# Turning normed tokens and key features through a DRAM scratch and VectorE's 32x32 blocks, in a window-attention plus linear-attention plus recurrence kernel

## The chip, the core and the metric

The kernel runs on one core of one Trainium2 chip, in float32 throughout. A core has TensorE (PE, matrix products; its weight loads are listed apart as PEld), VectorE (DVE), ScalarE (ACT), GpSimd (POOL) and SyncE (SP, which here only issues DMA transfers). The metric is the device time of one execution in microseconds (us), taken as the median of several runs.

## What is computed

The input is `x` with shape (16, 56, 56, 128): 16 images of 56x56 = 3136 tokens with 128 channels. Cut to what matters:

```python
# layer 0: shifted 7x7 window attention, 4 heads of 32, on a group-normed image
x = x + window_attention(group_norm(x)) @ w_out + b_out
# layer 1, on tokens t of shape (16, 3136, 128)
n = layer_norm(t)                      # over the 128 channels
q, k, v = split(n @ W.T + b)           # 128 channels each
q, k = elu(q) + 1, elu(k) + 1          # the "features"
num = q_t . cumsum_t(k_t v_t^T);  den = q_t . cumsum_t(k_t)
t = t + num / (den + 1e-6)             # causal linear attention
m = layer_norm(t) @ Wf.T               # second norm
m = batch_norm(m) * gamma + beta       # over all 16*3136 tokens
y_t = sigmoid(m_t + V y_{t-1})         # recurrence over the tokens of an image
out = t + y
```

Both layer norms give normed tokens with tokens on the partitions. The products that follow need them with channels on the partitions, so each normed group has to be turned. The causal attention also needs the key features both ways: channels on partitions for the products with the queries, tokens on partitions for the running state `sum k v^T`.

## The kernel before

Images are worked one after the other, with overlap. An image is cut into 8 rows of windows (`window_row`) and 7 token groups (`token_group`): six full groups of 512 tokens (four chunks of 128) and a small one of 64. For a token group the work is:

- `project` (L1132, PE) and `plus_attention` (L1141, DVE) finish layer 0 in the token buffer `xt_buf`.
- `layer_scale` with key `a` makes the normed tokens: `stats` (L1031, DVE), `join` (L1038 to L1045, POOL), `scale` (L1051, POOL) into `xn`, then `turn`: four 128x128 PE transposes into a PSUM bank (by the helper at L620). `x_out` (L1160, ACT) copies the bank to `xnT`.
- `feature(1)` and `feature(0)` make key and query features `f1`, `f0`: product (L1173, PE), relu and exp (L1183, L1192, ACT), `larger` (L1196, DVE). `values` (L1221, PE) and `v_out` (L1230, DVE) make `v_buf`.
- `turn_k` (L1244, PE, four transposes) and `k_out` (L1248, ACT) give `k`, the key features with tokens on partitions. `products` (L1259, PE) multiplies keys with queries: `f1` is the operand that is loaded as weights.
- `attend` (L1288, L1291, PE) and `gather` (L1299, PE) use and extend the running state, which `copy_state` (L1311, ACT) takes out of PSUM after each chunk; `update` (L1368, DVE) adds the result to `xt_buf`, and `store` (L1092, SP) writes it to DRAM.
- `layer_scale` with key `f` does the second norm in the same way; `xf_out` (L1384, ACT) copies to `xfT`, `whole` (L1388, PE) multiplies, `xs_out` (L1405, ACT) lays the result into `staged`, and `store_inputs` (L1426, SP) writes one image of it to DRAM.

For images 1 to 15 the group norm's channels-first image is not made by PE: `load_turned` (L322, SP) loads the image into one of two buffers `spare` so that VectorE can turn it in 32x32 blocks (L654, seven instructions per image). After all images a second stage runs the recurrence over stored inputs (L1657 to L1722).

The order of the first stage is written by a planner. Each step has an engine, a cost and a delay in us (literals in the code), the steps it follows, and buffers that it takes and drops. `Plan.emit` runs a list schedule forwards and backwards up to 200 times with its own costs, keeps the shortest plan and emits all steps by planned start. On the chip each engine then works through its fixed order and waits where an input or a buffer is not ready; SP's transfers are in such a fixed order too. The steps compete for a few buffers: three PSUM banks (`b`), two pairs of banks (`a`), two `xn`, one each of `xnT`, `xfT`, `f0`, `f1`.

Of the kernel before, what the change touches and what calls it, by code (L numbers as in the profile page):

```python
# [11 lines left out]
ALU = mybir.AluOpType  # L12
# [14 lines left out]

TOL2 = 2.0 ** -38


# [24 lines left out]
class Plan:  # L55
# [97 lines left out]
    def forwards(self, rank):  # L153


        left = {tag: [(k, None) for k in range(n)] for tag, n in self.bufs.items()}
        users, where, behind = {}, {}, {}
        for s in self.steps:
            for d in s.drops:
                users.setdefault(d, []).append(s)  # L160
        count = {d: len(u) for d, u in users.items()}

        def begin(s):
            takes = [d for d in s.takes if d not in where]
            if not all(left[d.tag] for d in takes):
                return False
            for d in takes:
                where[d], before = left[d.tag].pop(0)
                if before is not None:
                    behind.setdefault(s.n, []).extend(users[before])  # L170
            return True

        def done(s):
            for d in s.drops:
                count[d] -= 1
                if not count[d]:
                    left[d.tag].append((where[d], d))

        start, end = self.run(
            [s.missing for s in self.steps],  # L180
            [s.then for s in self.steps],
            rank,
            [0.0] * len(self.steps),
            begin,
            done,
        )
        if any(t is None for t in start):
            return None
        return start, end, where, behind
# [16 lines left out]
    def emit(self):  # L206
        best = now = self.forwards([s.rank for s in self.steps])
        assert best is not None
        for i in range(self.PASSES):
            back = self.backwards(*now[:2], now[3], self.AHEAD[i % len(self.AHEAD)])  # L210
            now = self.forwards([-t for t in back])
            if now is None:
                break
            if now[1] < best[1]:
                best = now
        start, self.span, where, _ = best
        for d, place in where.items():
            d.place = place

        for s in sorted(self.steps, key=lambda s: start[s.n]):  # L220
            s.emit()
# [3 lines left out]
def tile_conv_attn_hybrid(  # L225
# [52 lines left out]
    x3_d = dram.tile([B * T, C], F32, name="x3_d")  # L278
    xs_d = dram.tile([NJ, P, B - 1, KB, NCH], F32, name="xs_d")


# [133 lines left out]
    with ExitStack() as s1:  # L415
# [14 lines left out]
        def own(buf, *shape):  # L430
# [4 lines left out]
            return owned[key]  # L435

        NQ2 = 64 + WT
        psum = bass.MemoryType.PSUM
# [45 lines left out]
        for xt in xt_bufs:  # L484
# [6 lines left out]
                **{f"xt{i}": 1 for i in range(3 * NG)},  # L491
                "spare": 2,
                "oT": 1,
# [55 lines left out]
        def load(b, rank, paced):  # L549
# [17 lines left out]
            for g in range(NG):  # L567
# [12 lines left out]
                def emit(g=g):  # L580
# [4 lines left out]
                        "SP",  # L585
                        2.0 if g < NG - 1 else 0.7,
                        rank + g,
                        emit,
                        after,
                        takes=[bufs[g]],  # L590
                        lag=6.0,
                    )
# [6 lines left out]
        def load_turned(b, rank):  # L599

            buf = Buf("spare")
            parts = []
            for q in range(4):
                parts.append(
                    plan.step(
                        "SP",
                        5.0,
                        rank + q,
                        lambda q=q: load_blocks(b, spare[buf.place], q),
                        [issued, *parts[-1:]],  # L610
                        takes=[buf],
                        lag=12.0,
                    )
                )
            return buf, parts
# [22 lines left out]
        def turned(b, t, loaded, xw_buf, rank):  # L638
# [10 lines left out]
            for j in range(NG if b else 0):  # L649
                rk = rank + SLOT * 6.0 * j / NG  # L650

                def turn_rows(j=j):
                    n = R * W
                    nc.vector.transpose(  # L654
                        image_rows(xw_buf)[:, R * j : R * (j + 1), 0:W],
                        flat(spare[xp.place])[:, n * j : n * (j + 1)],
                    )
# [358 lines left out]
        last_pd = [[], []]  # L1016
        chain = {"state": None, "kept": None, "buf": None, "project": None, "turn": None}

        def layer_scale(t, g, d, key, rank, after, drops=()):

# [3 lines left out]

            end = key == "f" and t["b"] == B - 1 and g >= NG - 2

            def stats():
# [20 lines left out]

            def scale():
                d["xn"] = own(xn, P, G, C)[:, :nk]  # L1050
                (nc.vector if end else nc.gpsimd).tensor_tensor(  # L1051
                    d["xn"][:np],
                    xg,
                    d["rs"].unsqueeze(2).to_broadcast([np, nk, C]),
                    ALU.mult,
                )

            def turn():
# [5 lines left out]

            xn, bt = Buf("xn"), Buf("b")
            s = plan.step("DVE", part(g, (0.78, 0.87), (0.20, 0.28)), rank, stats, after)
# [9 lines left out]
                drops=drops,  # L1076
            )
            s = plan.step(
                "PE",
# [6 lines left out]
            )  # L1086
            return s, bt, sc

        def store(b, g, t, done, xt_buf, rank):

            def emit():
# [6 lines left out]
                    "SP",  # L1098
                    part(g, 2.0, 0.7),
                    rank,  # L1100
                    emit,
                    [done],
                    drops=[xt_buf],
                    lag=5.5,
                )
            )

        def token_group(b, g, i, t, turned_x, rows_done, oT_buf, xt_buf, rank):
# [46 lines left out]
            s = st("DVE", part(g, (0.61, 0.69), (0.20, 0.28)), rank, plus_attention, [s0, s1], drops=[bo])  # L1155
            s, bt, scaled = layer_scale(t, g, d, "a", rank, [s])

            def x_out():
                d["xnT"] = own(xnT, P, GT)
                nc.scalar.copy(d["xnT"][:, :nt], d["pt"])  # L1160

            xnT = Buf("xnT")
            xo = st("ACT", part(g, (0.47, 0.58), (0.11, 0.22)), rank, x_out, [s], takes=[xnT], drops=[bt])

            def feature(j):
# [3 lines left out]
                def proj():  # L1171
# [3 lines left out]
                        awc_sb[:, j * P : (j + 1) * P],  # L1175
                        d["xnT"][:, :nt],
                        start=True,
# [16 lines left out]
                def larger():  # L1194
                    d[key] = own(f, P, GT)
                    nc.vector.scalar_tensor_tensor(  # L1196
                        d[key][:, :nt],
                        d[f"p{j}"],
                        bqk_one[:, j : j + 1],
                        d[f"r{j}"],  # L1200
                        ALU.add,
                        ALU.max,
                    )
# [13 lines left out]
            def values():  # L1217
                pv = bank(bv, P, nk, C)
                d["pv"] = pv[:np]
                for cc in range(nk):  # L1220
                    nc.tensor.matmul(  # L1221
                        pv[:, cc, :],
                        chunk(d["xnT"], cc),
                        awc_sb[:, 2 * P : 3 * P],
# [21 lines left out]
            def k_out():  # L1246
                d["k"] = own(k, P, G, C)
                nc.scalar.copy(d["k"], d["pk"])  # L1248

            bk, k, bA, A = Buf("b"), Buf("k"), Buf("b"), Buf("A")  # L1250
            if g < NG - 1:
                s = st("PE", (0.44, 0.61), rank, turn_k, [fk], takes=[bk], drops=[bfk])
# [3 lines left out]
            def products():  # L1256
                d["pA"] = bank(bA, P, nk, np)
                for cc in range(nk):
                    nc.tensor.matmul(  # L1259
                        d["pA"][:, cc, :],  # L1260
                        chunk(d["f1"], cc),
                        chunk(d["f0"], cc)[:, :np],
# [116 lines left out]
            store(b, g, t, up, xt_buf, rank)  # L1379
            s, bt, scaled = layer_scale(t, g, df, "f", rank, [up], [xt_buf])  # L1380

            def xf_out():
                d["xfT"] = own(xfT, P, GT)[:, :nt]
                nc.scalar.copy(d["xfT"], df["pt"])  # L1384

            def whole():
                d["pw"] = bank(bw, P, nt)
                nc.tensor.matmul(d["pw"], fwTc_sb, d["xfT"], start=True, stop=True)  # L1388

# [18 lines left out]

            last = b == B - 1 and g == NG - 1
            bw, xfT = Buf("b"), Buf("xnT" if last else "xfT")  # L1410
            s = st("ACT", part(g, (0.47, 0.58), (0.11, 0.22)), rank, xf_out, [s], takes=[xfT], drops=[bt])
            s = st("PE", part(g, (0.86, 1.02), (0.17, 0.33)), rank, whole, [s], takes=[bw], drops=[xfT])
# [11 lines left out]
        def store_inputs(b, t, done, rank):  # L1424
            def emit():
# [5 lines left out]
            return plan.step(  # L1431
                "SP", 5.8, rank, emit, done, drops=[t["xs_buf"]], lag=10.0
            )
# [75 lines left out]
        def fetch(kind, m, first, last, after, tag=None):  # L1509
            def emit():  # L1510
                if tag is not None and tag[:2] == "xt":
                    ahead[kind][m] = xt_bufs[int(tag[2:])]
                elif tag is not None:
                    ahead[kind][m] = {
                        "spare": spare,
                        "xw": xw_bufs,
# [6 lines left out]
            elif tag[:2] == "xt":  # L1523
                takes = [Buf(f"xt{NG * int(tag[2:]) + g}") for g in range(NG)]
            else:
                takes = [Buf(tag)]
# [5 lines left out]
        def xs_until(b):  # L1532
# [4 lines left out]
            (M2, f"xt{(B - 2) % 3}"),  # L1537
            (0, "spare"),
            (1, "spare"),
        )  # L1540
# [333 lines left out]
```

## Time and profile before

| what | us |
|---|---|
| median of 3 runs | 1758.76 (1757.2 to 1760.62) |
| the profiled execution | 1757.42 |
| its span, first to last instruction | 1755.6 |
| first stage (0 to 1592): PE, PEld busy | 1572.39, 1302.99 |
| first stage: DVE, ACT, POOL busy | 1207.82, 1125.62, 1148.60 |
| recurrence (1592 to 1755.6): DMA share | 0.95 |

The granted TensorE clock is 0.996 of full speed. A row of instruction groups in the profile reads: line, engine, operation, output and inputs by name, shapes and count, then total busy us and mean ns of one, then the engine's idle time just before and who ended it. A duration is from start to end of one instruction; instructions of an engine overlap in part, so the distance between two starts can be well below the duration. "DMA share" is the mean busy share of the 16 DMA engines.

### The profile page before, as it was taken

Reading aid. Unit: us, or ns where it says so; the run is one execution under the profiler, and the core shown is the slowest. Engines: PE = TensorE matmul, PEld = TensorE weight load, DVE = VectorE, ACT = ScalarE, POOL = GpSimd, SP = SyncE. Lnnn points to the kernel's source line nnn. Section 1 sums busy time; section 2 is a strip of 40 time slices with the busy share of each in tenths; the row PEclk is TensorE's granted clock in tenths of the full one; section 3 lists DMA queues with packets and bytes.
Section 4 is the critical chain, followed back from the end, with each engine's and each line's share of the span. In section 5 each row is a group of like instructions: output and inputs, shape, how many; then the busy total and the mean of one; then the engine's idle time right before and its main releaser. Section 6 shows DMA issues by size and latency. Waiting matters only on the chain.

```text
span 1755.6 us, 63643 instructions
## 1 busy us (share of the span) xinstructions
PE 1719.7 (98%) x26539; PEld 1419.7 (81%) x26539; DVE 1350.2 (77%) x3174; ACT 1230.0 (70%) x3026; POOL 1152.7 (66%) x2042
## 2 busy tenths in 40 slices
PE   7999999999999999999999999999999999999997
PEld 6888888888878888888888888888888888786875
DVE  5888687686868687776878687777868677767997
ACT  5676676777767677767677677767677676766764
POOL 6887777767768687767777687768767676662000
PEclk9999999999999999999999999999999999999998
DMA  8244323132323223131323223231211020357999
GB/s 176 52 94 97 65 71 74 40 88 56 89 56 77 68 69 71 47 92 45 91 54 76 63 67 72 64 83 38 70 37 59 20 89 26 119 172 295 400 419 367
DMA packets 340391, 180.38 MB, mean 103 GB/s; under 512 B 194560, under 2 KB 323840, under 8 KB 338304
## 3 DMA queue, kind: packets, MB, share of 16 engines
q1 hardware_dynamic: 338512, 175.46, 33.9%
q8 instruction: 210, 3.44, 0.8%
q10 hardware_dynamic: 1584, 0.79, 0.1%
q14 instruction: 85, 0.70, 0.1%
HBM read 100.76 MB, written 75.46 MB: 100 GB/s over the span
## 4 chain that ended last, share of the span: by engine, by line
PE 89%; DVE 5%; DMA 3%; issue 2%; POOL 1%; ACT 1%; SPq 0%; DVEq 0%; POOLq 0%; ACTq 0%
PE bank L835 10%; PE bank L1173 10%; PE bank L856 7%; PE pair L880 6%; PE pair L935 5%; PE bank L620 5%; PE pair L954 5%; PE state_bank L1299 5%; PE bank L1259 5%; PE bank L1132 5%; PE pair L1288 5%; PE bank L1221 5%; PE pair L1291 5%; PE bank L1388 5%; PE bank L1244 2%; PE z_buf L1669 2%
## 5 line engine op out<-in xcount | busy, mean ns | idle before, releaser
L925 POOL TENSOR_TENSOR p_buf<-p_buf,rc 128x784 f32<-128x784 f32 x128 | 194.7, 1522 | 101.4 <-DVE rc L922 52.5
L906 POOL TENSOR_TENSOR s<-s,mx 128x784 f32<-128x784 f32 x128 | 192.5, 1504 | 60.8 <-DVE mx L903 56.4
L1173 PE MATMUL bank<-xnT,awc_sb 128*128 128x512 f32 (+1 forms) x448 | 210.1, 550 | 1.2 <-issue 1.2
L1183 ACT ACTIVATE r<-bank,bqk_neg 128x512 f32<-128x512 f32 (+1 forms) x224 | 142.6, 637 | 96.7 <-PE bank L1173 81.1
L1196 DVE SCALAR_TENSOR_TENSOR f<-bank,bqk_one,r 128x512 f32<-128x512 f32 (+1 forms) x224 | 150.2, 671 | 73.6 <-ACT r L1192 39.1
L1288 PEld LDWEIGHTS pair<-state,f 128*128 128x128 f32 x768 | 124.7, 191 | 45.1 <-issue 27.0
L920 DVE TENSOR_REDUCE sm<-p_buf 128x16 f32<-128x784 f32 x128 | 122.6, 958 | 45.3 <-ACT p_buf L916 44.8
L1291 PE MATMUL pair<-v_buf,A 128*128 128x129 f32 x800 | 155.3, 275 | 2.0 <-issue 1.8
L1299 PE MATMUL state_bank<-v_buf,k 128*128 128x129 f32 x768 | 153.8, 282 | 0.7 <-ACT k L1248 0.5
L891 DVE TENSOR_TENSOR s<-pair,wmask_sb 128x784 f32<-128x784 f32 x128 | 123.1, 962 | 40.5 <-PE pair L880 32.8
L1299 PEld LDWEIGHTS state_bank<-v_buf,k 128*128 128x128 f32 x768 | 122.4, 191 | 36.4 <-issue 21.6
L1288 PE MATMUL pair<-state,f 128*128 128x129 f32 x768 | 151.7, 279 | 0.0
L1311 ACT COPY state<-state_bank 128x129 f32<-128x129 f32 x384 | 105.9, 276 | 62.3 <-PE state_bank L1299 55.0
L945 ACT COPY pT<-pair 128x904 f32<-128x904 f32 x128 | 118.2, 923 | 28.7 <-PE pair L935 25.7
L1672 ACT ACTIVATE y_a<-z_buf,bsh 128x256 f32<-128x256 f32 (+1 forms) x218 | 103.3, 474 | 45.9 <-PE z_buf L1669 41.9
L1121 POOL TENSOR_TENSOR xt_buf<-xt_buf,bout_sb 128x512 f32<-128x512 f32 (+1 forms) x112 | 129.7, 1161 | 5.7 <-DMA xt_buf<-in_x_dram 5.7
L1192 ACT ACTIVATE r<-r 128x512 f32<-128x512 f32 (+1 forms) x224 | 131.0, 585 | 2.2
L1669 PE MATMUL z_buf<-y_a,fvT_sb 128*128 128x256 f32 (+1 forms) x432 | 129.7, 385 | 0.5 <-ACT y_a L1672 0.4
L880 PEld LDWEIGHTS pair<-kT,q_buf 32*49 32x49 f32 x8192 | 105.5, 120 | 27.5 <-issue 15.3
L620 PE MATMUL bank<-ident,xn 128*128 128x128 f32 x800 | 124.9, 274 | 2.1 <-issue 1.0
L1291 PEld LDWEIGHTS pair<-v_buf,A 128*128 128x128 f32 x800 | 121.5, 192 | 3.3 <-issue 2.4
L880 PE MATMUL pair<-kT,q_buf 32*49 32x49 f32 x8192 | 121.8, 206 | 2.3 <-issue 2.3
(159 smaller groups left out, 4773.0 us busy)
## 6 DMA issues: line engine op xcount, KB each, us to landing
x_d<-xt_buf SPq DMA_DIRECT2D x96, 256.0 KB, 2.3
xt_buf<-in_x_dram SPq DMA_DIRECT2D x93, 256.0 KB, 2.8
spare<-in_x_dram SPq DMA_DIRECT2D x60, 392.0 KB, 4.6
xs_d<-staged SPq DMA_DIRECT2D x15, 1568.0 KB, 6.5
out_dram<-xw_buf SPq DMA_DIRECT2D x6, 1792.0 KB, 19.2
x_ring<-x_d SPq DMA_DIRECT2D x5, 1792.0 KB, 16.9
xw_buf<-x_d SPq DMA_DIRECT2D x4, 1792.0 KB, 14.8
out_dram<-x_ring SPq DMA_DIRECT2D x4, 1792.0 KB, 17.0
```

The costliest lines, as they stand in the source:

```text
L620: nc.tensor.transpose(pt[:, CK * cc : CK * (cc + 1)], xg[:, cc, :], ident)
L835: nc.tensor.matmul(d[key], wqkv_sb[:, j * P : (j + 1) * P], xk, start=True, stop=True)
L880: nc.tensor.matmul(sc[64 * hh : 64 * hh + WT, hp, w * WT : (w + 1) * WT], qT[r : r + HD, w * WT : (w + 1) * WT], d["kT"][r : r + HD, w * W ...
L906: nc.gpsimd.tensor_tensor(d["sf"], d["sf"], d["mx"].unsqueeze(2).to_broadcast([P, nb, WT]), ALU.subtract,)
L925: nc.gpsimd.tensor_tensor(prf, prf, d["rc"].unsqueeze(2).to_broadcast([P, nb, WT]), ALU.mult)
L1173: nc.tensor.matmul(d[f"p{j}"], awc_sb[:, j * P : (j + 1) * P], d["xnT"][:, :nt], start=True, stop=True,)
L1183: nc.scalar.activation(d[f"r{j}"], d[f"p{j}"], AF.Relu, bias=bqk_neg[:, j : j + 1], scale=-1.0,)
L1196: nc.vector.scalar_tensor_tensor(d[key][:, :nt], d[f"p{j}"], bqk_one[:, j : j + 1], d[f"r{j}"], ALU.add, ALU.max,)
L1288: nc.tensor.matmul(to, chunk(d["f0"], cc), t["states"][c], start=True, stop=False)
L1291: nc.tensor.matmul(to, d["A"][:, cc, :], v1[:, cc, :], start=c == 0, stop=True)
L1299: nc.tensor.matmul(t["pd"], d["k"][:, cc, :], v1[:, cc, :], start=c == 0, stop=True, skip_group_check=True,)
L1669: nc.tensor.matmul(z, fvT_sb, y_prev, start=False, stop=True, skip_group_check=True)
```

## The change

Images 0 to 14 and full groups only (`blocks_moved`); the last image and the small groups keep the old way. Three turnings per group are concerned, with keys `a`, `f` and `k`.

- `scale` writes the normed group in another order: the four 32-channel quarters outermost. It goes to one of three places `xm` cut from the second `spare` buffer. For the key features `larger` writes `f1` with the four chunks innermost, so that neighbouring tokens of a chunk lie four floats apart.
- `through_dram` sends the group to a DRAM scratch (one transfer of 256 KB, 512-byte pieces), waits for it to land, and brings it back with four transfers of 64 KB, one for each 32 destination partitions, into one of four places `xp`, also in the second `spare` buffer.
- One VectorE instruction (`turn_blocks`) turns the 32x32 blocks straight into `xnT`, `xfT` or `k`. The PE transposes and the ACT copies of these groups are gone.
- `products` reads its weights from the chunk-innermost `f1` with a step of four floats.
- `load_turned` has one `spare` buffer instead of two.
- The planner's costs and delays for DMA steps are smaller, and its search goes on with shaken ranks where it used to stop.

```diff
+KEYS = ('f', 'a', 'k')
...
+    xn_d = {
+        key: dram.tile([B - 1, NG - 1, 4, P, P], F32, name=f"xn{key}_d") for key in KEYS
+    }
...
+        AT_SPARE = {"xm": 0, "xp": 3}
+        def at_spare(buf):
+            k = AT_SPARE[buf.tag] + buf.place
+            return flat(spare[1])[:, GT * k : GT * (k + 1)]
...
-                "spare": 2,
+                "spare": 1,
+                "xm": 3,
+                "xp": 4,
...
+        def blocks_moved(key, b, g):
+            return key in KEYS and b < B - 1 and g < NG - 1
+        def through_dram(key, b, g, src, xp, rank, after, drops):
+            there = xn_d[key][b, g]
+            def away():
+                nc.sync.dma_start(
+                    there.rearrange("s p r -> p s r"),
+                    src().rearrange("p (s r) -> p s r", s=4),
+                )
+            def back():
+                for s4 in range(4):
+                    nc.sync.dma_start(
+                        at_spare(xp)[32 * s4 : 32 * (s4 + 1)].rearrange(
+                            "i (q r) -> i q r", q=4
+                        ),
+                        there[s4].rearrange("(q i) r -> i q r", q=4),
+                    )
+            s = plan.step("SP", 0.7, rank, away, after, drops=drops, lag=2.6)
+            return plan.step("SP", 1.6, rank, back, [s], takes=[xp], lag=3.6)
...
             def scale():
+                if blocks:
+                    d["xm"] = at_spare(xn)
+                    nc.gpsimd.tensor_tensor(
+                        d["xm"].rearrange("p (q k c) -> p k q c", q=4, k=G),
+                        xg.rearrange("p k (q c) -> p k q c", q=4),
+                        d["rs"].unsqueeze(2).unsqueeze(3).to_broadcast([P, G, 4, 32]),
+                        ALU.mult,
+                    )
+                    return
...
+            def turn_blocks():
+                d["xT"] = own(to, P, GT)
+                nc.vector.transpose(
+                    d["xT"].rearrange("p (k s i) -> p k s i", k=G, s=4),
+                    at_spare(xp).rearrange("p (q k c) -> p k q c", q=4, k=G),
+                )
...
+            if blocks:
+                s = through_dram(key, t["b"], g, lambda: d["xm"], xp, rank, [sc], [xn])
+                s = plan.step("DVE", (0.59, 0.68), rank, turn_blocks,
+                    [s, chain[key]], takes=[to], drops=[xp])
...
                 def larger():
                     d[key] = own(f, P, GT)
+                    to, a1, a2 = d[key][:, :nt], d[f"p{j}"], d[f"r{j}"]
+                    if j and blocks_moved("k", b, g):
+                        to = to.rearrange("p (c k) -> p k c", k=G)
+                        a1 = a1.rearrange("p (k c) -> p k c", k=G)
+                        a2 = a2.rearrange("p (k c) -> p k c", k=G)
...
+            def turn_blocks():
+                d["k"] = own(k, P, G, C)
+                nc.vector.transpose(
+                    d["k"].rearrange("p k (q c) -> p k q c", q=4),
+                    at_spare(xp).rearrange("p (q c k) -> p k q c", q=4, k=G),
+                )
+            def keys(cc):
+                if blocks_moved("k", b, g):
+                    return d["f1"].rearrange("p (c k) -> p k c", k=G)[:, cc]
+                return chunk(d["f1"], cc)
```

## The prediction

> **What bounds the kernel now.** I read the page's head, the slices, the chain, then the groups by shape, the windows, SP's own waits and the transfers. The head, two slice rows and the chain's engine and line rows:
>
> ```profile
> PE 1719.7 (98%) x26539; PEld 1419.7 (81%) x26539; DVE 1350.2 (77%) x3174; ACT 1230.0 (70%) x3026; POOL 1152.7 (66%) x2042
> ...
> PE   7999999999999999999999999999999999999997
> ...
> DMA  8244323132323223131323223231211020357999
> ...
> PE 89%; DVE 5%; DMA 3%; issue 2%; POOL 1%; ACT 1%; SPq 0%; DVEq 0%; POOLq 0%; ACTq 0%
> PE bank L835 10%; PE bank L1173 10%; PE bank L856 7%; PE pair L880 6%; PE pair L935 5%; PE bank L620 5%; PE pair L954 5%; PE state_bank L1299 5%; PE bank L1259 5%; PE bank L1132 5%; PE pair L1288 5%; PE bank L1221 5%; PE pair L1291 5%; PE bank L1388 5%; PE bank L1244 2%; PE z_buf L1669 2%
> ```
>
> PE is busy nearly without a gap for the first nine tenths, and the chain that ended last runs on PE for 89%, transposes (L620, L1244) included. So time taken off PE there shortens the run, until another engine takes over. The end (DMA row 7999) is the recurrence, bound by transfers; the change doesn't touch it. The two stages as windows (busy us of PE, PEld, DVE, ACT, POOL, then clock, DMA share, GB/s), with two inner stretches:
>
> ```profile
> 0.00:1592.00 1592.00, 1572.39 (x25685) 1302.99 (x25686) 1207.82 (x2937) 1125.62 (x2806) 1148.60 (x2032) 1.00 0.29 74
> 1592.00:1755.60 163.60, 147.26 (x855) 116.70 (x853) 142.38 (x238) 104.40 (x221) 4.05 (x11) 0.97 0.95 384
> ...
> 100.00:1500.00 1400.00, 1394.12 (x22925) 1157.21 (x22924) 1070.11 (x2610) 1002.82 (x2503) 1017.55 (x1783) 1.00 0.26 65
> ...
> 1300.00:1400.00 100.00, 98.75 (x1678) 82.30 (x1677) 74.87 (x187) 71.61 (x183) 65.75 (x124) 1.00 0.14 43
> ```
>
> PE is busy 98.8% of 1592 us, DVE 76%, DMA 29%. DVE is the reserve that the change spends.
>
> **What it removes.** 15 images x 6 groups x 3 keys = 270 turnings. Their price, from a stretch of the timeline of weight loads (start, us, count) and the groups by shape:
>
> ```profile
> 650.98 0.47 PEld L620 LDWEIGHTS bank<-ident,xn 128*128 128x128 f32 x4
> 651.41 0.97 PEld L856 LDWEIGHTS bank<-wqkv_sb,oT_buf 128*128 128x128 f32 x8
> ```
>
> ```profile
> L620 PE MATMUL bank<-ident,xn 128*128 128x128 f32 x800 | 124.9, 274 | 2.1 <-issue 1.0 <-DVE xn L1051 0.6 <-ACT v L868 0.4
> L1160 ACT COPY xnT<-bank 128x512 f32<-128x512 f32 x96 | 56.7, 590 | 18.2 <-PE bank L620 17.9 <-DVE rc L922 0.2
> L654 DVE STREAM_TRANSPOSE xw_buf<-spare 128x448 f32<-128x448 f32 x105 | 63.0, 622 | 0.0
> ```
>
> A PE transpose lasts 274 ns, but four follow each other in 651.41 - 650.98 = 0.43 us, 0.11 us each; the rest is pipeline. 270 x 4 x 0.11 = **119 us off PE**. On ACT 270 copies of 0.59 us go, 159 us; ACT is only 71% busy, so I count nothing for it. Three PSUM banks also see less traffic.
>
> **What it adds on DVE.** The nearest row is L654: 63.0/105 = 0.60 us for 448 elements. The 512- and 64-element forms of L1196 (738 and 268 ns) give 470/448 = 1.05 ns per element, so 512 cost 0.60 + 0.07 = 0.67 us, and 270 of them **180 us**. Each waits for four transfers; the built program has 486 more separate wait instructions on DVE. They last 21 to 50 ns: 10 to 24 us if exposed, 0 if beside running work; I take 10. DVE goes to 1208 + 180 + 10 = 1398 us, and PE's stage to 1592 - 119 = 1473: DVE would be 95% busy. Nearly all the reserve is gone before any stride is counted.
>
> Here the skill speaks against the change. VectorE: DVE Perf Modes, "Rules for kernel authors", sends a 128x128 transpose to TensorE wherever PSUM will do as destination, as it does here; its table under "The three transpose paths" has 390 ns on TensorE against 311 on VectorE (bf16). By the table's TensorE price 1080 transposes would be worth 421 us. By the trace they are worth 119, and DVE pays 180. The trace decides: the exchange is good only because PE is full and DVE isn't.
>
> **The stride.** Key features lie chunk innermost, so three operations step by 16 bytes: `larger` for keys writes so (90), the turning for `k` reads so (90), `products` loads weights so (360 products, two loads each). No such operation is in the trace. The nearest rows are ACT's copies into single columns of `staged`, whose step is 128 bytes, beside a dense copy:
>
> ```profile
> L1405 ACT COPY staged<-bank 128x88 f32<-128x88 f32 x16 | 5.3, 334 | 0.0
> ...
> L1405 ACT COPY staged<-bank 128x64 f32<-128x64 f32 x16 | 4.4, 274 | 1.0 <-PE bank L1388 1.0
> ...
> L1160 ACT COPY xnT<-bank 128x64 f32<-128x64 f32 x16 | 3.5, 222 | 1.1 <-PE bank L620 0.7 <-PE bank L1221 0.4
> ...
> L1405 ACT COPY staged<-bank 128x12 f32<-128x12 f32 x16 | 3.1, 194 | 0.0
> ```
>
> Between 12 and 88 elements a stepped copy costs (334 - 194)/76 = 1.84 ns per element; dense, (590 - 222)/448 = 0.82. So stepping about doubles the element's price. The skill, Advanced Engine Details and Errata, "SBUF Cachelines", says that SBUF lines have 16 bytes, that it takes at least two hits on a line for full speed, and that a new line at each access is penalised: at a step of 16 bytes each access is a new line, so all three pay. SBUF — State Buffer, on the same lines, names four fp32 as how far one can stride for free: nothing is paid. By the first DVE pays 180 x 512 x 1.05 ns = 97 us and PE, whose loads sit 0.11 us apart, 720 x 0.11 = 79 us; by the second 0 and 0. For DVE I take the full 97, the ACT row being near; for weight loads no row is near, and I take half, 40. DVE then needs 1398 + 97 = 1495, PE 1473 + 40 = 1513.
>
> **The scratch.** Per turning SP issues five transfers, 1350 in all, 0.37 us each as the median of those issued now. That is 500 us of SP's own time, beside some 360 transfers now; SP now idles for long spells, so issue itself is covered. The transfers (KB each, median us to landing) and SP's longest waits:
>
> ```profile
> x_d<-xt_buf SPq DMA_DIRECT2D x96, 256.0 KB, 2.3
> ...
> spare<-in_x_dram SPq DMA_DIRECT2D x60, 392.0 KB, 4.6
> xs_d<-staged SPq DMA_DIRECT2D x15, 1568.0 KB, 6.5
> ```
>
> ```profile
> SPq L1092 <- DVE xt_buf L1368: 523.9, 67, 36.4
> ...
> SPq L310 <- DMA x_d<-xt_buf: 151.5, 70, 6.8
> ```
>
> Way out 2.3 us (same size and piece as x_d), way back 3 x 0.37 of issue plus some 2.1 for the last quarter: 5.5 us, against about 1.2 us for PE transpose and copy. Traffic: 270 x 2 x 262 KB = 142 MB, 103 GB/s over 1380 us. The window 1300 to 1400, which has no 128-byte pieces in it, moves 43 GB/s at a share of 0.14, so the share rises by 0.33, from 0.26 to 0.6. Not full, but a transfer will often stand behind a `spare` load (4.6 us) or the store of `staged` (6.5). SP issues in order: `back` waits at its head for `away` to land, and behind it stand the next `away`, loads and stores. The built program also lets a transfer wait for the eighth before it, as there are eight completion semaphores in turn.
>
> What covers a late transfer is the order. Laying trace durations on the after program's fixed order, 8.7 us of DVE work (median; least 5.1, lower quarter 7.2) stands between `larger` for keys and the turning of `k`, for a round trip of 5.5 plus wake-ups. On PE 13 us of work (median) stand between the key product and its first `gather`, for a chain of about 9.4: relu 0.69, exp 0.64, larger 0.74, trip 5.5, turn 0.67 and hops. So 2 to 4 us of lateness are hidden in the middle case, little in the lower quarter, and a stalled DVE at 95% cannot catch up. Bounds: 0 if all is hidden, 270 x 0.5 = 135 us if each turning stalls DVE half a microsecond. I take 0.15 us each, **40 us**, for this and for two nearly full engines in lockstep.
>
> What I cost at nothing: the POOL `scale` (L1051, 1041 ns) in another order, POOL being 72% busy (90 x 2 x 0.2 us = 36 us if short runs hurt it, still hidden); the single `spare`, as the next image's four loads take about 18 us of a 98 us image and follow the seven L654; the planner's search, which reorders everything, worth at most the 20 us that PE idles now.
>
> **Sum**, against the profiled 1757.4 (span 1755.6 and 1.8 around it): -119 + 40 + 40 = -39, so 1718; the median shown is 1.3 us above the profiled run: **1720 us**, its own range 1695 to 1752.
>
> **Rivals.** *Full gain*: steps of 16 bytes are free and lateness is covered. PE 1473 with 0 to 30 of friction: 1640 to 1690, about 1660. For: SBUF page's sentence, the reserve in SP and DMA. Against: the ACT row.
> *Both strides at full*: PE 1473 + 79 = 1552, DVE 1495, 94 to 97% of each other; with 40 of friction the stage is back at 1592: 1757, spread 1735 to 1785. The gain is used up by keys alone.
> *Slower, by late transfers*: the place is `turn_blocks` in DVE's queue; behind it wait masks, maxima and sums of the window rows, and PE behind those. After the -79 net of stride, 270 turnings use the gain up at 79/270 = 0.29 us of stall each. At 0.4 to 0.5 (108 to 135 us) the time is 1788 to 1815, about 1795. For: a share of 0.6, one in-order queue, 6.5 us stores among trips with 2 to 3 us of slack. Against: the orders' slack on PE is about as large as now, where PE hardly idles.
> *It doesn't do what it says* is out: the built program has 1080 PE transposes and 270 ACT copies fewer.
>
> **Chances.** Partial gain 0.30, full gain 0.17, both strides 0.24 (faster 0.02, within 0.2% 0.06, slower 0.16), late transfers 0.29. 0.2% is about what runs of this kernel can tell from no change. Faster 0.30 + 0.17 + 0.02 = 0.49, same 0.06, slower 0.45. The range 1655 to 1815 leaves out half of the full gain's low side and the worst of late transfers.
>
> **What would show it.** Right: L620 at about 105 transposes and L1244 at 24; DVE at 94% or more of the first stage; the key form of L1196 near 1.27 us; DVE idle before the turnings small; DMA share near 0.6. Wrong towards faster: L1196 still 0.74 us and the 16-byte weight loads still 0.11 apart. Wrong towards slower: landings of the scratch above 4 us each way, large idle time on DVE ended by DMA, SP waiting for its own transfers, and PE idle behind masks and features.

## The result, and the profile after

The changed kernel takes 1766.29 us (median of 9 runs, 1761.33 to 1770.61) against 1758.76 us (9 runs, 1756.98 to 1760.62) on the same chip: a ratio of 1.0042 [1.0027, 1.0057]. It is slower by 7.5 us. The forecast was 1720 us and faster, so it was wrong in direction. The time lies in the range, in the case called *both strides at full* (1735 to 1785).

The profiled execution took 1766.56 us. The head of its page, two slice rows and the chain by engine:

```profile
PE 1704.9 (97%) x25459; PEld 1396.5 (79%) x25459; DVE 1555.7 (88%) x3444; ACT 1098.6 (62%) x2756; POOL 1152.1 (65%) x2042
...
PE   7899999999999999999999999999999999999997
...
DMA  5466667666575757565564747566655435457999
...
PE 62%; DVE 12%; DMA 11%; POOL 6%; SPq 4%; issue 4%; ACT 1%; DVEq 0%; POOLq 0%
```

PE has 1080 matrix instructions fewer, yet it is busy only 15 us less (1704.9 after 1719.7). And the chain, which lay on PE for 89%, now runs through DVE, the transfers and SP's sequencer for 27%. So two things have to be explained: PE work that came back, and a new kind of waiting.

The two stages as windows (busy us of PE, PEld, DVE, ACT, POOL, then clock, DMA share, GB/s). The recurrence starts at about 1600 us here, some 9.5 us later than before, so the whole loss is in the first stage:

```profile
0.00:1592.00 1592.00, 1550.38 (x24565) 1274.85 (x24565) 1408.11 (x3189) 989.79 (x2525) 1142.32 (x2014) 0.99 0.60 161
1592.00:1764.80 172.80, 154.54 (x897) 121.70 (x895) 147.56 (x256) 108.76 (x232) 9.74 (x28) 0.98 0.94 376
```

The groups by shape that the change touches (key products, `larger`, the three turnings):

```profile
L1375 PEld LDWEIGHTS bank<-f,f 128*128 128x128 f32 x800 | 188.7, 312 | 21.8 <-DVE f L1287 7.9 <-issue 5.5 <-DVE rd L1480 1.0
...
L1287 DVE SCALAR_TENSOR_TENSOR f<-bank,bqk_one,r 128x512 f32<-128x512 f32 x192 | 177.4, 924 | 12.7 <-PE pair L1404 6.0 <-ACT r L1278 4.0 <-ACT q_buf L862 0.8
...
L1343 DVE STREAM_TRANSPOSE k<-spare 128x512 f32<-128x512 f32 x90 | 100.1, 1112 | 26.1 <-DMA spare<-xnk_d 25.7
...
L1129 DVE STREAM_TRANSPOSE xnT<-spare 128x512 f32<-128x512 f32 x90 | 63.1, 702 | 20.8 <-DMA spare<-xna_d 14.6 <-PE bank L1312 5.2 <-PE bank L1259 1.0
L1129 DVE STREAM_TRANSPOSE xfT<-spare 128x512 f32<-128x512 f32 x90 | 62.9, 699 | 8.2 <-DMA spare<-xnf_d 7.1 <-DMA spare<-xnk_d 0.8
```

A dense turning of 512 elements takes 0.70 us, the stepped one for `k` 1.11. The rows end with who released DVE: nearly always the transfers that bring the group back. DVE's list of waits (total us, times, longest) puts them together, 47 us in 54 waits:

```profile
DVE k L1343 <- DMA spare<-xnk_d: 25.7, 26, 3.1
...
DVE xnT L1129 <- DMA spare<-xna_d: 14.6, 18, 1.9
...
DVE xfT L1129 <- DMA spare<-xnf_d: 7.1, 10, 1.6
```

The weight loads of one group's key products in the timeline (start, us, then what, eight loads), first in the changed kernel, then in the first experiment below, where the steps of 16 bytes are gone:

```profile
605.59 1.94 PEld L1375 LDWEIGHTS bank<-f,f 128*128 128x128 f32 x8
```

```profile
602.16 0.97 PEld L1371 LDWEIGHTS bank<-f,f 128*128 128x128 f32 x8
```

A weight load that steps by 16 bytes takes twice the time of a dense one: 0.24 us for 0.12. On 90 groups of eight loads that is 90 x 0.97 = 87 us; the group's busy time gives 188.7 - 103.2 (the dense run) = 85 us.

The transfers of the page (KB each, median us to landing), and one row of SP's timeline (start, us) in which the four transfers that bring a group back are issued:

```profile
x_d<-xt_buf SPq DMA_DIRECT2D x96, 256.0 KB, 2.9
...
xs_d<-staged SPq DMA_DIRECT2D x15, 1568.0 KB, 7.2
xna_d<-spare SPq DMA_DIRECT2D x90, 256.0 KB, 2.9
spare<-xna_d SPq DMA_DIRECT2D x360, 64.0 KB, 2.1
xnk_d<-f SPq DMA_DIRECT2D x90, 256.0 KB, 2.6
```

```profile
602.21 2.13 SPq L1057 DMA_DIRECT2D spare<-xna_d  x4
```

Landing suffered little while the DMA share doubled (0.29 to 0.60): the same `x_d` store went from 2.3 to 2.9 us. But SP takes its time. The four transfers of the row take 2.13 us; over all 270 trips it is 1.73 at the least, 1.9 in the middle and over 3.7 in one of twenty. The 90 trips of `k` in SP's timeline take 5.3 us in the middle from the issue of the way out to the end of the fourth issue back (least 4.0, upper quarter above 6.1). That issue (0.43) begins a landing of 2.1, so 1.7 more are to come: by this estimate a trip is 7.0 us in the middle, 5.7 at the least, above 7.8 in the upper quarter. For eleven of these trips the trace also has the last landing itself: 6.9 us in the middle. The sum had 5.5; the planner's delays, counted from the start of each step, are 2.6 + 3.6 = 6.2.

### The profile page after: what moved, and what is told of

It reads as the page before. It is cut to its first block, busy times and chain, and to the rows that moved or that the text cites. A ratio compares the mean times of both kernels' runs of the same rounds, so it can differ in the third digit from the quotient of the medians.

```text
span 1764.8 us, 63537 instructions
## 1 busy us (share of the span) xinstructions
PE 1704.9 (97%) x25459; PEld 1396.5 (79%) x25459; DVE 1555.7 (88%) x3444; ACT 1098.6 (62%) x2756; POOL 1152.1 (65%) x2042
## 4 chain that ended last, share of the span: by engine, by line
PE 62%; DVE 12%; DMA 11%; POOL 6%; SPq 4%; issue 4%; ACT 1%; DVEq 0%; POOLq 0%
PE bank L1375 8%; PE bank L1259 7%; PE bank L857 7%; PE bank L878 5%; PE pair L902 4%; SPq L1057 4%; PE pair L957 4%; PE state_bank L1415 4%; PE bank L1502 4%; PE pair L976 4%; PE bank L1312 3%; PE pair L1404 3%; PE pair L1407 3%; PE bank L1224 3%; DVE z_buf L1773 2%
## 5 line engine op out<-in xcount | busy, mean ns | idle before, releaser
L1259 PE MATMUL bank<-xnT,awc_sb 128*128 128x512 f32 (+1 forms) x448 | 213.8, 560 | 1.8 <-DVE v_buf L1321 0.6
L1375 PEld LDWEIGHTS bank<-f,f 128*128 128x128 f32 x800 | 188.7, 312 | 21.8 <-DVE f L1287 7.9
L1287 DVE SCALAR_TENSOR_TENSOR f<-bank,bqk_one,r 128x512 f32<-128x512 f32 (+1 forms) x224 | 185.8, 829 | 14.3 <-PE pair L1404 6.0
L1375 PE MATMUL bank<-f,f 128*128 128x128 f32 (+1 forms) x800 | 192.8, 382 | 3.6 <-DVE f L1287 3.2
L1415 PEld LDWEIGHTS state_bank<-v_buf,k 128*128 128x128 f32 x768 | 124.8, 192 | 52.3 <-issue 24.4
L938 ACT ACTIVATE p_buf<-s 128x784 f32<-128x784 f32 x128 | 112.6, 880 | 20.1 <-POOL s L928 19.8
```

Source lines behind the costliest of these rows:

```text
L1259: nc.tensor.matmul(d[f"p{j}"], awc_sb[:, j * P : (j + 1) * P], d["xT"][:, :nt], start=True, stop=True,)
L1287: nc.vector.scalar_tensor_tensor(to, a1, bqk_one[:, j : j + 1], a2, ALU.add, ALU.max,)
L1375: nc.tensor.matmul(d["pA"][:, cc, :], keys(cc), chunk(d["f0"], cc)[:, :np], start=True, stop=True,)
L1415: nc.tensor.matmul(t["pd"], d["k"][:, cc, :], v1[:, cc, :], start=c == 0, stop=True, skip_group_check=True,)
```

## The experiments

Each ratio is to the kernel before, timed beside it. Its medians were 1757.36, 1759.01 and 1757.26 us in the three batches (r1 to r4, r5 to r8, r9 to r12).

### 1. The steps of 16 bytes taken away

Order, transfers and instruction counts stay; only the views change. The key state then mixes tokens, so this kernel, r2 and r3 compute something else with work of the same size.

```diff
 def larger():
-    if j and blocks_moved("k", b, g):
-        to = to.rearrange("p (c k) -> p k c", k=G)
-        a1 = a1.rearrange("p (k c) -> p k c", k=G)
-        a2 = a2.rearrange("p (k c) -> p k c", k=G)
 def turn_blocks():   # for k
-    at_spare(xp).rearrange("p (q c k) -> p k q c", q=4, k=G),
+    at_spare(xp).rearrange("p (q k c) -> p k q c", q=4, k=G),
 def keys(cc):
-    return d["f1"].rearrange("p (c k) -> p k c", k=G)[:, cc]
+    return chunk(d["f1"], cc)
```

> The changed kernel with the same order and the same transfers, but no 16-byte steps: larger writes the key features densely, products loads its weights densely, the turning of k reads densely. The quarters sent through the scratch then hold the wrong tokens, so the key state is computed from mixed tokens; the amount of work is the same. Theory A (the 16-byte steps used the gain up): weight loads go back from 0.23 to 0.11 us apart (720 loads, 86 us off PE), DVE gets 180 x 0.40 = 73 us back, time 1665 to 1700. Theory B (late scratch transfers and a full DVE queue used it up): DVE still waits about 47 us for the scratch and the time falls by 30 us at most, 1735 to 1766.

Measured: 1715.46 us, 0.9768 [0.9743, 0.9792], between the ranges of the two theories. Its groups by shape:

```profile
L1283 DVE SCALAR_TENSOR_TENSOR f<-bank,bqk_one,r 128x512 f32<-128x512 f32 x192 | 139.7, 728 | 9.9 <-PE pair L1400 4.6 <-ACT r L1278 3.9 <-ACT staged L1515 0.8
...
L1371 PEld LDWEIGHTS bank<-f,f 128*128 128x128 f32 x800 | 103.2, 194 | 25.1 <-issue 8.9 <-DVE f L1283 7.3 <-DVE rd L1476 1.0
...
L1339 DVE STREAM_TRANSPOSE k<-spare 128x512 f32<-128x512 f32 x90 | 63.4, 705 | 49.1 <-DMA spare<-xnk_d 49.0
```

The three steps together cost 85 us of weight loads, 37.7 us in `larger` and 36.7 us in the turning of `k`, but 1766.3 - 1715.5 = 51 us of time. The rest of what came free went into waiting, as the last row tells: DVE now stands 49.0 us before the turnings of `k`, where it stood 25.7. Its waits on the scratch:

```profile
DVE k L1339 <- DMA spare<-xnk_d: 49.0, 36, 5.0
...
DVE xfT L1129 <- DMA spare<-xnf_d: 20.6, 21, 2.4
DVE xnT L1129 <- DMA spare<-xna_d: 19.1, 23, 2.2
```

That is 89 us for 47. The chain is on PE for 41% only, on DVE for 20, transfers for 18, SP's sequencer for 8. So the steps are a main cause, but they hide a second one behind them. Neither theory holds alone.

### 2 and 3. PE's step alone, DVE's two alone

```diff
 # r2: as r1, but keys() keeps its step
+    return d["f1"].rearrange("p (c k) -> p k c", k=G)[:, cc]
 # r3: as the changed kernel, but keys() is dense
-    return d["f1"].rearrange("p (c k) -> p k c", k=G)[:, cc]
+    return chunk(d["f1"], cc)
```

> As the kernel without steps, but products loads its weights with the step of 16 bytes (of wrong tokens); DVE works densely. Same order. Theory A: PE carries its 86 us, DVE is relieved of 73: if PE's loads are the larger part, 1735 to 1760; if DVE's two operations are, 1690 to 1715. Theory B: little different from the changed kernel, 1750 to 1766.

> As the changed kernel, but products loads its weights densely (of wrong tokens); larger and the turning of k keep the step of 16 bytes. Same order. Theory A with PE as the limit: 1690 to 1720, DVE busy near 97% of the first stage at its end. Theory A with DVE as the limit: 1735 to 1766. Theory B: within 10 us of the changed kernel.

Measured: PE's step alone 1744.04 us, 0.9922 [0.9905, 0.9938]; DVE's two alone 1735.30 us, 0.9881 [0.9865, 0.9898]. Over r1 that is 28.6 and 19.8 us, together 48 of the 51: in this order, with the trips late, the two effects add. r2 lies in the range for PE's loads as the larger part, r3 at the lower edge of the one for DVE as the limit, though its chain is on DVE for only 24%. The group rows of r2 show the doubled loads again:

```profile
L1371 PEld LDWEIGHTS bank<-f,f 128*128 128x128 f32 x800 | 189.0, 312 | 18.5 <-issue 6.3 <-DVE f L1283 3.6 <-DVE rd L1476 0.7
```

In r2 DVE's waits on the scratch are 50.5 us, in r3 54.4, where r1 has 88.7. The reading is that a slower engine gives the trips more time, so that 85 us of PE work cost only 28.6 as long as the trips are late.

### 4. A complete kernel without the steps

`larger` writes densely, an ACT copy lays the key features into a place `xm` with the quarters outermost, and that goes to the scratch; products and turning are as in r1. It computes what the changed kernel computes, at the price of 90 copies on ACT.

```diff
-                xp = Buf("xp")
-                s = through_dram("k", b, g, lambda: d["f1"], xp, rank, [fk], [bfk])
+                xp, xk = Buf("xp"), Buf("xm")
+                def quarters():
+                    d["km"] = at_spare(xk)
+                    nc.scalar.copy(
+                        d["km"].rearrange("p (s k c) -> p k s c", s=4, k=G),
+                        d["f1"].rearrange("p (k s c) -> p k s c", k=G, s=4),
+                    )
+                s = st("ACT", (0.53, 0.63), rank, quarters, [fk], takes=[xk], drops=[bfk])
+                s = through_dram("k", b, g, lambda: d["km"], xp, rank, [s], [xk])
```

> Complete kernel without steps: larger writes densely, ACT copies the key features once more with token quarters outermost (90 copies of about 0.64 us, runs of 128 bytes), the scratch takes that copy, products loads densely, the turning of k reads densely. The planner orders anew. Theory A: 1670 to 1705, as without steps, since ACT is only 62% busy. Theory B: the trip for k is one hop and about 0.8 us longer, so 1760 to 1800.

Measured: 1711.74 us, 0.9740 [0.9710, 0.9770], about as r1 and 7 us above the range of theory A. The steps can be avoided at no visible price, ACT being 66% busy with the copies (62% in the changed kernel). What is left is lateness: 87.5 us of DVE's waits are on the scratch.

```profile
DVE k L1339 <- DMA spare<-xnk_d: 44.9, 36, 3.7
...
DVE xfT L1129 <- DMA spare<-xnf_d: 24.0, 23, 2.4
...
DVE xnT L1129 <- DMA spare<-xna_d: 18.6, 18, 2.1
```

### 5 and 6. Fewer keys through the scratch

```diff
-KEYS = ('f', 'a', 'k')
+KEYS = ('f', 'a')     # r5
+KEYS = ()             # r6
```

> Only the two normed groups (keys a and f) go through the scratch; key features are turned on PE as before, densely. 720 transposes and 180 copies are saved instead of 1080 and 270, DVE gets 120 us instead of 180. Theory C (without steps the trip of the key features is the next bound, since the state chain waits for it with the least cover): DVE's waits for the scratch fall from 89 us (no steps) below 45, and 79 us less PE work shows nearly whole: 1685 to 1705, no slower than the kernels without steps although PE does 40 us more. Theory D (the rest is lost to a full DVE and load on the transfers in general, k being no special case): 1720 to 1735.

> No key goes through the scratch: what is left of the change is the planner's search and its costs for transfers, and the single spare buffer. Expected within 8 us of the kernel before (1750 to 1766); if the planner or the single buffer cost the gain, above 1770.

Measured: normed tokens alone 1698.04 us, 0.9649 [0.9633, 0.9666]; none at all 1750.43 us, 0.9952 [0.9935, 0.9969]. So the planner's new search and costs, with the single `spare`, are worth 8 us by themselves, within the 20 foretold. The normed tokens bring 52 more, although 36 us of waits on the scratch remain (24.4 for `xfT`, 11.7 for `xnT`). And `k`, as the change does it, takes 68 us away again: 1766.3 against 1698.0.

### 7. The longer delays told to the planner

r4 with delays of 3.4 + 4.8 = 8.2 us, which cover about three of four trips as measured. Nothing but the order changes:

```diff
-            s = plan.step("SP", 0.7, rank, away, after, drops=drops, lag=2.6)
-            return plan.step("SP", 1.6, rank, back, [s], takes=[xp], lag=3.6)
+            s = plan.step("SP", 0.7, rank, away, after, drops=drops, lag=3.4)
+            return plan.step("SP", 1.9, rank, back, [s], takes=[xp], lag=4.8)
```

> The complete kernel with the ACT copy, with the planner told longer trips (way out 3.4 us instead of 2.6, way back 4.8 instead of 3.6, its issue 1.9 instead of 1.6), so that more work stands between a trip and its use. Theory C/D alike (late transfers): DVE's waits for the scratch fall from 88 us to below 45 and the time to 1680 to 1700. If lateness isn't what is left: 1705 to 1725.

Measured: **1658.54 us, 0.9438 [0.9420, 0.9456]**, the lowest median of all, better than both kernels and 21 us below the range expected. Its page's head and chain:

```profile
PE 1612.1 (97%) x25458; PEld 1306.9 (79%) x25459; DVE 1488.8 (90%) x3444; ACT 1134.1 (69%) x2846; POOL 1148.9 (69%) x2042
...
PE 80%; DVE 7%; DMA 5%; POOL 2%; issue 2%; ACT 2%; SPq 1%; DVEq 0%; POOLq 0%; ACTq 0%
```

And its waits on the scratch, 20.9 us for r4's 87.5:

```profile
DVE xfT L1129 <- DMA spare<-xnf_d: 8.2, 7, 2.9
DVE k L1339 <- DMA spare<-xnk_d: 6.5, 9, 1.5
DVE xnT L1129 <- DMA spare<-xna_d: 6.2, 4, 2.3
```

PE is busy 107.6 us less than before, the time fell by 100; 8 of the 100 came with the planner alone (r6). DVE, at 90%, is not the bound: the chain is on PE again for 80%. The longer delays are worth 53 us here (1711.7 to 1658.5). They work through the distance in the fixed orders: in the middle case 10.0 us lie between the start of the ACT copy and the turning of `k` in r4's trace, waits included, and 11.0 in r7's, where hardly a wait is left. The trips themselves did not get shorter: to the end of the fourth issue back they take 5.8 us in r4 and 6.3 in r7.

### 8. The true costs, without the delays

The planner of the changed kernel is told the measured prices of the stepped operations.

```diff
 # larger for moved keys (0.65, 0.74) -> (1.03, 1.14); turning of k, products:
-(0.59, 0.68) ... (0.89, 1.05)
+(1.00, 1.10) ... (1.84, 2.03)
```

> The changed kernel with all its steps, with the planner told what the stepped operations cost (larger for keys 1.03 us instead of 0.65, the turning of k 1.00 instead of 0.59, products 1.84 instead of 0.89). If a plan made on wrong costs was a part of the loss: 1735 to 1755. If the work itself is the cause: 1757 to 1772.

Measured: 1796.89 us, 1.0216 [1.0199, 1.0233], 31 us slower than the changed kernel and the opposite of what was expected. Its waits on the scratch have doubled to 97 us:

```profile
DVE k L1343 <- DMA spare<-xnk_d: 48.2, 41, 4.4
DVE xfT L1129 <- DMA spare<-xnf_d: 28.4, 26, 2.8
DVE xnT L1129 <- DMA spare<-xna_d: 20.8, 18, 2.7
```

One would think that, with dearer work in the plan, fewer instructions seem enough to cover a trip. The trace does not bear this out: between `larger` for keys and the turning of `k` DVE runs 19 instructions in the middle case in both kernels, and is busy with them 7.7 us in the changed kernel and 7.8 in r8 (at the least 4.6 and 4.0). The trips of `k` became a little longer (5.7 for 5.3 us to the end of the fourth issue), which is little for 31 us. Why this order is so much later stays open. That longer delays cure it is shown next.

### 9 to 12. Delays with and without the rest

r9: the changed kernel with r7's delays only. r10: r8 with them. r11: r5 with them. r12: r7 with 4.2 and 6.0 in place of 3.4 and 4.8.

> The changed kernel with its steps of 16 bytes, and only the planner's delays of the trip changed (way out 3.4 us instead of 2.6, back 4.8 instead of 3.6, its issue 1.9 instead of 1.6). In the order the DVE work between larger and the turning of k rises from 8.7 us (median) to 11.0. Theory E (steps and late trips are two separate losses): DVE's 47 us of waits for the scratch fall below 25 and the time to 1725 to 1750. If the steps alone hold the kernel back: 1757 to 1770.

> The changed kernel with the true costs of the stepped operations and the longer delays. Theory E with the true costs harmful only because the tighter plan left the trips late: DVE's waits for the scratch fall from 97 us below 45, 1725 to 1755, about as with the longer delays alone. If the true costs harm by themselves: above 1775.

> Only keys a and f through the scratch, with the longer delays. The waits for the scratch are 36 us with the short ones and PE holds 80% of the chain: 1675 to 1695. Below 1658 it would be the best version, and key features would not belong in the scratch at all.

> The complete kernel with the ACT copy, planned with still longer delays (4.2 and 6.0 us). Waits for the scratch are 21 us with 3.4 and 4.8: little is left to gain, 1648 to 1662; if longer holds of the few buffers f0, f1 and xm begin to bind: 1665 to 1700.

| kernel | median us | ratio [95%] | DVE's waits on the scratch, us |
|---|---|---|---|
| the changed kernel | 1766.29 | 1.0042 [1.0027, 1.0057] | 47.4 |
| r9: with longer delays | 1740.83 | 0.9906 [0.9889, 0.9922] | 9.8 |
| r8: with true costs | 1796.89 | 1.0216 [1.0199, 1.0233] | 97.4 |
| r10: with both | 1734.08 | 0.9870 [0.9853, 0.9886] | 11.5 |
| r4: ACT copy, no steps | 1711.74 | 0.9740 [0.9710, 0.9770] | 87.5 |
| r7: r4 with longer delays | 1658.54 | 0.9438 [0.9420, 0.9456] | 20.9 |
| r12: r4 with still longer ones | 1662.62 | 0.9467 [0.9451, 0.9482] | 2.5 |
| r5: normed tokens alone | 1698.04 | 0.9649 [0.9633, 0.9666] | 36.1 |
| r11: r5 with longer delays | 1687.05 | 0.9602 [0.9586, 0.9618] | 5.5 |

DVE's waits on the scratch in r9, where nothing but the delays differs from the changed kernel:

```profile
DVE xfT L1129 <- DMA spare<-xnf_d: 4.1, 3, 3.1
DVE k L1343 <- DMA spare<-xnk_d: 3.2, 3, 2.0
DVE xnT L1129 <- DMA spare<-xna_d: 2.5, 2, 1.7
```

Between `larger` for keys and the turning of `k` DVE now runs 24 instructions in the middle case instead of 19, and is busy with them 10.0 us instead of 7.7. In all four pairs the longer delays take most of the waits away and make the kernel faster: by 25 us as the change stands, by 53 without steps, by 63 with true costs, by 11 without `k`. Each pair also has two different orders, and a new search alone was worth 8 us (r6); so 53 and 63 are clear of the luck of an order, 11 barely. For the same reason the 7 us by which true costs help once the delays are longer (1740.8 to 1734.1) are not shown to be theirs. Beyond r7's delays nothing is won: r12 has 18 us less of waits and no better time. `k` pays only densely and covered: 1658.5 against 1687.0, 28 us; stepped and covered it loses 54 (1740.8 against 1687.0).

So the account, from r7 to the change: without steps and with covered trips -100 us; the steps +82 (r7 to r9, the ACT copies going in exchange); the late trips +25 (r9 to the changed kernel). Together +7.5, as measured. This is one way of dividing it. Taken in the other order, late trips cost 53 (r7 to r4) and the steps 55 (r4 to the change): the two losses hide each other in part, and only their sum, 108 us, is fixed. That PE's loads are most of the 82 was not separated with covered trips; their 85 us on an engine that the chain is on for 75% in r9 speak for it.

## Point by point

**Off PE: 119 us.** Nearly right. r7 gained 100, 92 of them over r6, with PE's busy time down by 107.6; L642 and L1335, the transposes of the changed kernel, have 105 and 24 left as foretold. The 390 ns that the Trainium skill has for TensorE (VectorE: DVE Perf Modes, "The three transpose paths") would have promised 421.

**On DVE: turnings of 0.67 us, 95% busy.** The turning took 0.70. But DVE's busy time in the first stage rose by only 200 us (1207.8 to 1408.1, 88%) where 287 were summed. As durations the turnings and the longer `larger` make 226 + 38 = 264 us; over the whole span the durations of all DVE instructions rose by 254 us and its busy time by 205, so that some 50 to 60 us overlap with neighbours. The prediction read PE's transposes by the distance of their starts (0.11 for 274 ns) and DVE's by duration: two yardsticks in one sum. In no run does the chain lie on DVE for more than 24% (r3).

**The stride: the step that failed.** For weight loads no row was near, and the prediction took half of full price, 40 us. They cost all of it and a little more: 85, where full price was reckoned at 79. With 85 in that place the same sum gives -119 + 85 + 40 = +6, so 1757.4 + 6 + 1.3 = 1765 us, 1.6 from the measured time. That it comes so close is partly luck: in the account above the three parts are -100, +82 and +25, so an error of 19 in the first and one of 15 in the last cancel. The sign turns in r9 too, where only the trips are covered (1740.8). But lateness stood in the sum with 40, more than the 25 that r9 recovers; the term that was too small is the stride. For DVE the full 97 us were taken; 74 were measured. They were not in the sum, as PE was the longer of the two, though r3 shows that they cost 20 us alone. Of the two pages of the Trainium skill weighed there, Advanced Engine Details and Errata, "SBUF Cachelines", is borne out in that all three operations pay; that lines of 16 bytes are the reason no run shows, for no smaller step was tried. The sentence of SBUF — State Buffer that four fp32 can be strided for free is not borne out at this step. It was also no real counterweight: its own paragraph asks for two hits on a line as well, and the prediction read the one figure alone. The ACT row named as nearest, stepped at 128 bytes, was close: 1.84 ns per element there, 1.05 + 0.41/512 = 1.85 on DVE. With no row near for weight loads, the far row of another engine was a better guide here than the middle between two ends.

**The scratch: 40 us for lateness.** In size about right: 47 us of waits, of which longer delays recover 25 us of time. Its make-up was not: landing was estimated well (2.6 to 2.9 out, 2.1 back), but what SP adds between was not. The 1350 issues took 725 us of SP, 0.54 each, where 500 were reckoned, and the trip is 7.0 us where 5.5 were taken. The cover was too kind as well: 5.1 at the least and 8.7 in the middle are sums of durations, and in the trace DVE is busy for 4.6 and 7.7 us there. And lateness was treated as fixed; it is a property of the order, which three numbers in the planner set. That term grows as the others shrink: 47 us of waits with steps, 88 without. Hence the *full gain* case, which had lateness covered, could not come from taking away the steps alone (1715), but came with both (1658.5, forecast about 1660).

**Late transfers as sole cause** (1788 to 1815) fell: DMA share 0.60 as foretold, median landings of 2.9 and 2.1 us where 4 each way had been named as the sign, and 0.18 us of stall per turning instead of 0.4 to 0.5. One sign did come: SP waits for its own transfers. Before it brings a group back it stands 233 us in all until the way out has landed, and 119 in r9:

```profile
SPq L1057 <- DMA xnk_d<-f: 103.5, 64, 4.0
...
SPq L1057 <- DMA xna_d<-spare: 78.4, 52, 3.6
...
SPq L1057 <- DMA xnf_d<-spare: 50.7, 42, 3.7
```

And r8 shows the case within reach: 97.4/270 = 0.36 us each, and 1797 us.

**The planner's search, at most 20 us:** 8.

The chances were 0.49 for faster against 0.24 for both strides. The evidence for the full price on one engine was taken as weak evidence for the other, and since 39 us of gain and 45 us of missing price are of one size, that one choice decided the sign.

## What to carry to other kernels

When a layout change makes an operand step, list every instruction that reads or writes it, weight loads included, and look at the step in bytes: at 16 bytes the weight loads here took double the time, and VectorE paid 0.8 ns per element more. A further copy on an engine with time to spare can be cheaper than a view that costs nothing to write. A round trip through DRAM is priced as landing under load plus the issue of all its transfers and the waits of the queue between, and its price must stand in whatever makes the order: with other costs corrected and this one not, the kernel here was slower.

## What the runs showed of the hardware

- Weight loads of float32 with a column step of 16 bytes: 1.94 us for eight, dense 0.97; 312 against 194 ns as the mean over the group.
- VectorE writing at that step: 0.42 us more for 512 elements (177.4 - 139.7 over 90); a 32x32 turning that reads at it: 0.41 more. The same 1.85 ns per element as ScalarE at a step of 128 bytes.
- With the DMA share at 0.60 instead of 0.29 a 256 KB store landed in 2.9 us instead of 2.3, and the 1.5 MB store in 7.2 instead of 6.5. In r9, at a share of 0.61, the 256 KB store took 2.5, so the order counts as well as the share.
- Four transfers issued in a row on SP took 1.73 us at the least, 1.9 in the middle: about as much as the landing of the last (2.1).
